# The gates of six groups computed after the scan in two-level block products, and the second stretch's layer norm in smaller steps

## The chip, the cores and the metric

The kernel runs on one core of a Trainium2 chip. The metric is the device time of one execution in microseconds. The core's engines run side by side and meet through semaphores: TensorE (PE, matmuls, with PEld for its weight loads), VectorE (DVE), ScalarE (ACT), GpSimd (POOL), and SyncE (SP), from which all of this kernel's transfers are issued in one queue.

## What is computed

A layer norm, then a Mamba-2 block and a LoRA mixture on the normed input, and the sum of all three. Everything is in fp32. With L = 2048 tokens and a model width of 1024, 64 heads of 64 channels, 8 groups:

```python
xn = layernorm(x)
proj = xn @ in_proj_w.T
gate, hbc, dt = proj[:4096], proj[4096:10240], proj[10240:]
xBC = silu(causal_conv4(hbc) + conv_bias)
x_, B, C = xBC                       # 64 heads x 64; 8 groups x 128 each
dt = softplus(dt + dt_bias); dA = exp(-exp(A_log) * dt)
state = state * dA_t + (dt_t * x_t) * B_t      # over t
y_t = state . C_t + D * x_t
yn = y * rsqrt(mean(y*y over a group's 512) + eps) * norm_weight
attn = (yn * silu(gate)) @ out_proj_w.T
ffn = xn @ W_base.T + b_base + 2 * lora(xn)    # 2 of 8 experts, rank 16
out = x + attn + ffn
```

The gate is a plain projection of the normed input: 4096 output channels, 512 of them per group. It is used only after the scan, as a factor on the normed y of the same channel and token.

## The kernel before

Channels lie on the 128 partitions, tokens along the free dimension. The tokens are cut into two stretches of 1024 (`s` = 0, 1); in `in_pairs` (line 557) each stretch's projections are computed in pairs of two 128-channel tiles by one level of Strassen-Winograd products. For the right-hand side (the normed input) the seven operands `op_0` to `op_6`, each 128 x (4 x 512), stay in SBUF for a whole stretch and are kept in DRAM as `xop_d`. `pair` (line 450) makes seven products of four matmuls 128 x 128 x 512; each fp32 matmul shows as two instructions. It is a generator that yields after each product: `products(n, side)` (line 591) advances it n times and runs the given side steps in between. After each product ACT or DVE evicts the bank: `s1` (line 474), `s16` (478), `s15` (482), and the four `quarter` calls (line 531 for the DVE ones), which store to DRAM. A bank `px` is written by products 6, 7 and 4, in the order 1, 6, 5, 2, 7, 3, 4. Left operands (weight sums) are formed on POOL in the first stretch (line 427), kept in DRAM and loaded again in the second.

A group has three pairs for the convolution's channels (names `x`) and two for the gate (`g`, evicted through SiLU to `gate_d`). The LoRA part's base product has four pairs per stretch (`b`). That makes 88 pairs in all, 616 products. The first five pairs run ahead, the last two (`POST`) after the scan.

The scan has 32 blocks (stretch, group, half of 512 tokens) of four slots (chunks of 128 tokens). The main loop (from line 983) sets how many products go into a slot by `plan` and `target`, a straight line through given points, and puts the scan's steps between them:

- `scan_a` for the next chunk: the decay scan `es` (DVE, line 688), the chunk's C.B product and transpose into bank "aux" (PE), the mask product `dab` (DVE, 709), the transposes of x into bank "aux" (PE, line 88), and `xdt`, `xdd` (ACT, 720 and 728; sixteen small instructions).
- `scan_b` for this chunk, after the slot's first product: `ps_y`, `ps_e`, `ps_st` (PE), `ecp` and `xg` (DVE, 769 and 770), the state's decay (POOL) and the state's sum (DVE, 784, from bank "st").
- `conv` for the next block in slots 1 and 2 (18 DVE instructions, line 646), `norm_squares` in slot 3, `norm_mean` and `norm_gate` in the next block's slot 0. `norm_gate` (line 818) multiplies by the gate (line 832; loaded in `load_gate`, line 791) and stores `y_d`.

The second stretch's input is normed during the first stretch, in four pieces of 256 tokens (`ln_next`, line 244, then `small`, line 297, for dt, decays and routing). A piece has three blocks. In the first of them it is loaded, normed and turned into operands within slots 1 to 3; `small` follows in slots of the other two. `ln_next` uses the four-buffer pool `ev`, which the evictions use too, and PSUM bank "st".

From block 15 on, POOL forms the output projection's weights for two levels (`out_sums`, line 866, from and to DRAM), one tile per block.

After the scan come the last two base pairs, and then the output projection (from line 1088): two levels of the same scheme. It has four passes (stretch, half of the groups) of seven units of seven products; here a product is eight matmuls of 256 columns. The stretches run in the order 1, 0. Right-hand quarters are loaded from `y_d`; sums for both levels are made on DVE.

Tiles are placed by a framework that inserts the semaphores; instructions marked `keep_in_program_order` (all matmuls and transposes among them) keep the order in which the code issues them.

Of the kernel before, what the change touches and what calls it, by code (L numbers as in the profile page):

```python
# [13 lines left out]
L = 2048  # L14
# [21 lines left out]
NW = 12  # L36
PRE = 5
# [5 lines left out]
def mamba_lora_kernel(  # L43
# [20 lines left out]
    const = ctx.enter_context(tc.tile_pool(name="const", bufs=1))  # L64
    in_ctx = ExitStack()
    op = in_ctx.enter_context(tc.tile_pool(name="op", bufs=1, side="right"))
# [177 lines left out]
    def ln_next(s, i):  # L244
# [4 lines left out]
        of = halved(flat, f"{s}_{i}", ev, "ev")  # L249
        yield  # L250
        ps = over_channels(of, "st", f"mean_{s}_{i}")
# [3 lines left out]
        sqs = []  # L255
        for h in range(2):
            normal(flat[:, 4 * h : 4 * h + 4, :], mean, ALU.subtract)
            for k in (4 * h, 4 * h + 2):
                sq = ev.tile([P, 2, 2 * Q], F32, tag="ev", name=f"lsq_{s}_{i}_{k}")
                nc.scalar.activation(sq, flat[:, k : k + 2, :], AF.Square)  # L260
                sqs.append(sq)
            nc.vector.tensor_tensor(sqs[2 * h], sqs[2 * h], sqs[2 * h + 1], ALU.add)
            if h:
                nc.vector.tensor_tensor(sqs[0], sqs[0], sqs[2], ALU.add)
            yield
        ps = over_channels([sqs[0][:, 0, :], sqs[0][:, 1, :]], "st", f"var_{s}_{i}")
# [4 lines left out]
        for h in range(2):  # L271
# [5 lines left out]
        t4, t1, t2, t3 = (  # L277
            ev.tile([P, KH, Q], F32, tag="ev", name=f"t_{s}_{i}_{j}") for j in range(4)
        )
        nc.vector.tensor_tensor(t1, b12, b11, ALU.subtract)  # L280
        nc.vector.tensor_tensor(t2, b22, t1, ALU.subtract)
        yield
        nc.vector.tensor_tensor(t4, b21, t2, ALU.subtract)
        nc.vector.tensor_tensor(t3, b22, b12, ALU.subtract)
# [12 lines left out]
    def small(s, i, chunks, sm, home):  # L297
# [7 lines left out]
        def tile(what, shape):  # L305
            pool, tag = home[what]
            return pool.tile(shape, F32, tag=tag, name=f"{what}_{n}")
# [25 lines left out]
        ps = ps_one.tile([P, nch, H], F32, tag="st", name=f"ps_tot_{n}")  # L333
# [223 lines left out]
    def in_pairs():  # L557
        for s in range(NS):
            ops = lambda s=s: ops_of["x", s]
            for g in range(G):  # L560
# [11 lines left out]
                for q in range(2):  # L572
# [14 lines left out]
    N_IN = NS * (5 * G + 4)  # L587
# [91 lines left out]
    def scan_a(s, g, half, c):  # L679
# [33 lines left out]
        pst = ps_one.tile([P, 4, Q], F32, tag="aux", name=f"ps_xt_{n}")  # L713
# [77 lines left out]
    def load_gate(s, g, half):  # L791
        sg = p1.tile([P, 4, TB], F32, tag="sg", name=f"sg_{s}_{g}_{half}")
# [25 lines left out]
    def norm_gate(s, g, half):  # L818
# [11 lines left out]
        for j in (0, 2):  # L830
            two = xg[:, j : j + 2, :]
            nc.vector.tensor_tensor(two, two, sg_of[s, g, half][:, j : j + 2, :], ALU.mult)
# [19 lines left out]
    def base_sums(pool, i):  # L852
# [7 lines left out]
        for j, what in ((3, "s1"), (4, "s2"), (5, "s3"), (6, "s4")):  # L860
            d = dram.tile([P, KH, P], F32, tag=f"{what}_b{i}", name=f"{what}_b{i}_d")
            nc.sync.dma_start(d, t[:, j])
            kept[f"b{i}", what] = d
        yield
# [107 lines left out]

    plan = [(0, 7 * PRE), (n_slots // 2 - NQ, 7 * (5 * G + 5)), (n_slots, total)]

# [433 lines left out]
```

## Time and profile before

| | us |
|---|---|
| median of three runs | 3438.68 (3438.17 to 3439.08) |
| the profiled execution | 3437.5 |
| its span, first to last instruction | 3435.7 |
| scan: first to last decay scan (L688) | 117.9 to 2644.9 |
| last one-level product begins | 2722.9 |
| first matmul of the output projection | 2726.3 |
| mean granted TensorE clock | 0.998 |

The span falls into a start of about 118 us, the scan of some 2530 us, the last base products, and the output projection of some 710 us. Transfers move 224 GB/s on average over the span. A busy time counts the stretches in which at least one instruction of the engine is under way; matmul instructions overlap, so the distance from one start to the next says more than the mean duration of one (592 ns for 512 columns). Waits are put down to what ended them last.

### The profile page before, as it was taken

Reading aid. Unit: us, or ns where it says so; the run is one execution under the profiler, and the core shown is the slowest. Engines: PE = TensorE matmul, PEld = TensorE weight load, DVE = VectorE, ACT = ScalarE, POOL = GpSimd, SP = SyncE. Lnnn points to the kernel's source line nnn. Section 1 sums busy time; section 2 is a strip of 40 time slices with the busy share of each in tenths; the row PEclk is TensorE's granted clock in tenths of the full one; section 3 lists DMA queues with packets and bytes.
Section 4 is the critical chain, followed back from the end, with each engine's and each line's share of the span. In section 5 each row is a group of like instructions: output and inputs, shape, how many; then the busy total and the mean of one; then the engine's idle time right before and its main releaser. Section 6 shows DMA issues by size and latency. Waiting matters only on the chain.

```text
span 3435.7 us, 38674 instructions
## 1 busy us (share of the span) xinstructions
PE 3404.6 (99%) x12820; PEld 1989.8 (58%) x12820; DVE 2410.5 (70%) x2733; ACT 1338.9 (39%) x3694; POOL 697.2 (20%) x443
## 2 busy tenths in 40 slices
PE   9999999999999999999999999999999999999999
PEld 7444544544545544544455454454454588888888
DVE  7547776877877867777777877777875466566665
ACT  2245454554555454545545455555453000000000
POOL 4123223222222211332222332222321000000000
PEclk9999999999999999999999999999999999999999
DMA  6546655655666676887778787877777777585654
GB/s 236 190 166 198 209 184 187 216 183 196 207 196 209 196 261 219 287 261 242 235 246 256 235 255 249 254 237 240 242 237 260 256 274 242 195 300 187 214 164 144
DMA packets 530327, 769.85 MB, mean 224 GB/s; under 512 B 35152, under 2 KB 264656, under 8 KB 527440
## 3 DMA queue, kind: packets, MB, share of 16 engines
q1 hardware_dynamic: 530128, 767.39, 68.7%
q8 instruction: 102, 1.67, 0.2%
q14 instruction: 97, 0.79, 0.1%
HBM read 516.64 MB, written 250.61 MB: 223 GB/s over the span
## 4 chain that ended last, share of the span: by engine, by line
PE 87%; DVE 8%; issue 2%; DMA 2%; ACT 2%; SPq 0%; DVEq 0%; ACTq 0%
PE ps_x_x L79 12%; PE ps_x_w L79 8%; PE ps_a_x L79 8%; PE ps_y_x L79 8%; PE ps_x_g L79 8%; PE ps_y_w L79 6%; PE ps_a_w L79 6%; PE ps_y_g L79 5%; PE ps_a_g L79 5%; PE ps_y L79 3%; PE ps_e L79 3%; PE ps_st L79 3%; PE ps_x_b L79 2%; DVE xg L646 2%; PE ps_a_b L79 2%
## 5 line engine op out<-in xcount | busy, mean ns | idle before, releaser
L83 POOL TENSOR_TENSOR state<-state,tot 128x512 f32<-128x512 f32 x112 | 150.2, 1341 | 1307.6 <-PE ps_e L79 1175.7
L688 DVE TENSOR_TENSOR_SCAN es<-dab,here 128x1024 f32<-128x1024 f32 x128 | 303.5, 2371 | 82.6 <-ACT xdd L728 81.3
L646 DVE SCALAR_TENSOR_TENSOR xg<-rawx,cw,xg 128x512 f32<-128x512 f32 x384 | 338.3, 929 | 16.8 <-ACT xg L640 15.9
L79 PE MATMUL ps_x_w<-t,w 128*128 128x256 f32 x1344 | 303.8, 379 | 0.0
L720 ACT ACTIVATE xdt<-ps_xt,dt 128x64 f32<-128x64 f32 x1024 | 223.0, 331 | 203.6 <-PE ps_xt L88 203.6
L79 PEld LDWEIGHTS ps_x_w<-t,w 128*128 128x128 f32 x1344 | 255.4, 190 | 41.5 <-issue 7.7
L705 ACT ACTIVATE ps_y<-xg,dsk 128x128 f32<-128x128 f32 x512 | 190.2, 371 | 222.5 <-DVE xg L770 192.9
L1345 ACT COPY s<-ps_a_w 128x512 f32<-128x512 f32 x28 | 16.4, 585 | 636.2 <-PE ps_a_w L79 555.6
L728 ACT ACTIVATE xdd<-xdt,es 128x64 f32<-128x64 f32 x1024 | 261.7, 387 | 0.0
L83 POOL TENSOR_TENSOR wo<-wo 128x512 f32<-128x512 f32 (+1 forms) x112 | 211.9, 1892 | 6.8
L709 DVE TENSOR_TENSOR dab<-es,cbm 128x1024 f32<-128x1024 f32 x128 | 177.6, 1388 | 39.3 <-ACT cbm L698 39.0
L79 PE MATMUL ps_a_w<-q,w 128*128 128x256 f32 x896 | 202.5, 379 | 0.0
L79 PEld LDWEIGHTS ps_a_w<-q,w 128*128 128x128 f32 x896 | 170.2, 190 | 23.6 <-issue 0.5
L79 PE MATMUL ps_x_x<-op_again,s_x 128*128 128x512 f32 x384 | 172.7, 592 | 0.0
L79 PE MATMUL ps_y_x<-op_again,s_x 128*128 128x512 f32 x384 | 172.7, 592 | 0.0
L79 PE MATMUL ps_a_x<-op_again,a_x 128*128 128x512 f32 x384 | 172.7, 592 | 0.0
L79 PEld LDWEIGHTS ps_y<-dab,xdt 128*64 128x64 f32 x2048 | 112.8, 137 | 102.9 <-issue 40.8
L79 PE MATMUL ps_x_x<-op,s_x 128*128 128x512 f32 x368 | 165.5, 592 | 0.0
L79 PE MATMUL ps_y_x<-op,s_x 128*128 128x512 f32 x368 | 165.5, 592 | 0.0
L79 PE MATMUL ps_a_x<-op,a_x 128*128 128x512 f32 x368 | 165.4, 592 | 0.0
L646 DVE SCALAR_TENSOR_TENSOR bc<-rawb,cw,bc 128x512 f32<-128x512 f32 x192 | 163.8, 885 | 1.9 <-ACT bc L640 1.3
L531 DVE TENSOR_TENSOR ev<-ps_x_x,s_x 128x512 f32<-128x512 f32 x94 | 64.4, 686 | 129.3 <-PE ps_x_x L79 124.2
(238 smaller groups left out, 6152.1 us busy)
## 6 DMA issues: line engine op xcount, KB each, us to landing
w<-w SPq DMA_DIRECT2D x196, 512.0 KB, 3.7
dab<-da_d SPq DMA_DIRECT2D x128, 512.0 KB, 5.4
raw<-ev SPq DMA_DIRECT2D x192, 256.0 KB, 3.3
a_x<-in_w_in_dram SPq DMA_DIRECT2D x168, 256.0 KB, 4.0
w<-wo SPq DMA_DIRECT2D x96, 448.0 KB, 4.3
ecp<-run_d SPq DMA_DIRECT2D x256, 128.0 KB, 4.0
gate<-ev SPq DMA_DIRECT2D x128, 256.0 KB, 3.6
sg<-gate SPq DMA_DIRECT2D x32, 1024.0 KB, 7.8
```

Source lines behind the costliest of these rows:

```text
L79: tc.keep_in_program_order(nc.tensor.matmul(*args, **kw))
L83: ins = nc.gpsimd.tensor_tensor(*args)
L531: nc.vector.tensor_tensor(e, ps, add, alu)
L646: nc.vector.scalar_tensor_tensor(dst[:, i, :], raw[:, i, k : k + TB], cw[:, ti, k : k + 1], dst[:, i, :], ALU.mult, ALU.add,)
L688: nc.vector.tensor_tensor_scan(es.rearrange("p h t -> p (h t)"), dab.rearrange("p h t -> p (h t)"), here, 0.0, ALU.mult, ALU.add,)
L705: nc.scalar.activation(psy[:, j, :], xg[:, j, cs], AF.Copy, scale=dsk[:, at : at + 1])
L709: nc.vector.tensor_tensor(ms, es, cbm.unsqueeze(1).to_broadcast([P, HG, Q]), ALU.mult)
L720: ins = nc.scalar.activation(xdt[:, h, :], x_t[:, h, :], AF.Copy, scale=dt_of[s][:, half * NQ + c, at : at + 1],)
L728: ins = nc.scalar.activation(xdd[:, h, :], xdt[:, h, :], AF.Copy, scale=es[:, h, Q - 1 : Q])
L1345: nc.scalar.copy(s1, pa)
```

## The change

It has two parts.

The first concerns the gates of groups 0 to 5 (`NO` = 3 pairs of groups). They leave `in_pairs`: 24 of the 88 pairs go, and `plan` is drawn anew for 64. `load_gate` does nothing for these groups, and `norm_gate` stores y without the gate. After the scan, during and behind the last base products, a new stage computes the gates: for each stretch and each two groups seven units (`gate_units`), each of them seven products of four matmuls of 256 columns. Left operands are read from `w_in` or from sums `s_d` that `oct_sums` forms on POOL, in blocks 30 and 31 and (the last third) in the new stage; the second level's left sums come from `left_two` (POOL), the right ones from `right_two` (DVE). The results gather in four tiles; `gated` applies SiLU (ACT), multiplies by y (DVE) and stores `yg_d`. The first stretch's operands are in place at the start; the second's are loaded again from `xop_d` towards the end of the first. The output projection then takes the stretches in the order 0, 1 and reads groups 0 to 5 from `yg_d`.

The second concerns the second stretch's layer norm. Each piece now takes twelve slots, from block 1 to block 12, with one or two steps per slot. It uses a scratch tile of its own (`scr`) in place of part of `ev`, and PSUM bank "aux" in place of "st"; `ps_xt`, the transposes of x in `scan_a`, moves from "aux" to "st". `out_sums` and the sums of the base weights begin one block earlier.

```diff
-                for q in range(2):
+                for q in range(2 if g >= 2 * NO else 0):
                     t = 4 * g + 2 * q
                     yield pair(
                         f"g{g}_{q}", f"g_{s}_{g}_{q}", halves(w_in[t], w_in[t + 1]), ops,
...
-        pst = ps_one.tile([P, 4, Q], F32, tag="aux", name=f"ps_xt_{n}")
+        pst = ps_one.tile([P, 4, Q], F32, tag="st", name=f"ps_xt_{n}")
...
-            nc.vector.tensor_tensor(two, two, sg_of[s, g, half][:, j : j + 2, :], ALU.mult)
+            if g >= 2 * NO:
+                nc.vector.tensor_tensor(two, two, sg_of[s, g, half][:, j : j + 2, :], ALU.mult)
...
-    plan = [(0, 7 * PRE), (n_slots // 2 - NQ, 7 * (5 * G + 5)), (n_slots, total)]
+    plan = [(0, 7 * PRE), (n_slots // 2 - NQ, 7 * (N_S + 4)), (n_slots, total)]
...
-            if after == 0 and c == 1:
+            i, at = divmod(4 * (b - 1) + c, 3 * NQ)
+            piece = (1, i)
+            if not (s == 0 and 0 <= i < NQ):
+                at = None
+            if at == 0:
                 load_piece(*piece, "sg", p1)
                 ln = ln_next(*piece)
-            if after == 0 and c == 2:
-                side += steps(ln, 3)
-            if after == 0 and c == 3:
-                side += steps(ln, 4)
-            if after == 1 and c in (0, 2, 3):
-                side += steps(rest, 1)
+            side += steps(ln, {2: 1, 3: 1, 4: 1, 5: 2, 6: 1}.get(at, 0))
+            side += steps(rest, {8: 1, 9: 1, 10: 1, 11: 2}.get(at, 0))
...
-            products(1, parts[3])
+            products(min(n - 3, 1), parts[3])
...
+    inner = (1, 6, 5, 2, 7, 3, 4)
+    HT = TB // 2
+    KQ = KH // 2
+    order = (1, 2, 6, 5, 7, 3, 4)
+    gate_units = [(s, o, i) for s in range(NS) for o in range(NO) for i in order]
...
+        add(s1, a21, a22, ALU.add)
+        yield
+        add(s2, s1, a11, ALU.subtract)
+        yield
+        add(s4, a12, s2, ALU.subtract)
+        yield
+        add(a21, a11, a21, ALU.subtract)
+        yield
...
+    def gated(s, o, a, n, z):
+
+        at = slice(s * TS + n * TB, s * TS + (n + 1) * TB)
+        y = gy.tile([P, 2, 2, TB], F32, tag="gy", name=f"gy_{s}_{o}_{a}{n}")
+        for q in range(2):
+            nc.sync.dma_start(y[:, q], y_d[2 * o + q][:, 2 * a : 2 * a + 2, at])
+        yield
+        for q in range(2):
+            nc.scalar.activation(z[:, q], z[:, q], AF.Silu)
+            yield
+        for q in range(2):
+            nc.vector.tensor_tensor(z[:, q], z[:, q], y[:, q], ALU.mult)
+            nc.sync.dma_start(yg_d[2 * o + q][:, 2 * a : 2 * a + 2, at], z[:, q])
+            yield
...
+        for n, j in enumerate(inner):
+            ps = {1: pa, 2: pa, 6: px, 7: px, 4: px, 5: py, 3: py}[j]
+            for q in range(2):
+                for k in range(KQ):
+                    mm(
+                        ps[:, q, :], left[j][:, q, k, :], right[j][:, k, :],
+                        start=(n < 3 and q + k == 0), stop=(k == KQ - 1), skip_group_check=True,
+                    )
...
-    passes = [(s, p) for s in (1, 0) for p in range(2)]
+    passes = [(s, p) for s in range(NS) for p in range(2)]
...
-            nc.sync.dma_start(x, y_d[4 * p + 2 * k + h][:, :, at : at + TB])
+            g = 4 * p + 2 * k + h
+            nc.sync.dma_start(x, (yg_d if g < 2 * NO else y_d)[g][:, :, at : at + TB])
```

## The prediction, made before the result was known

> **What bounds it now.** I read the busy shares first, then the order of matmuls on TensorE, then busy time in two stretches of the scan, then the waits.
>
> ```profile
> PE 3404.6 (99%) x12820; PEld 1989.8 (58%) x12820; DVE 2410.5 (70%) x2733; ACT 1338.9 (39%) x3694; POOL 697.2 (20%) x443
> ...
> 2667.09 3.60 PE L79 MATMUL ps_x_b<-op_again,s_b 128*128 128x512 f32 x8
> 2670.52 3.60 PE L79 MATMUL ps_y_b<-op_again,s_b 128*128 128x512 f32 x8
> ...
> 2729.77 3.62 PE L79 MATMUL ps_x_w<-t,w 128*128 128x256 f32 x16
> 2733.22 3.62 PE L79 MATMUL ps_y_w<-t,w 128*128 128x256 f32 x16
> ```
>
> PE is busy for 99% of the span, and products start one after the other without a gap: every 3.434 us for eight instructions of 512 columns, every 3.453 us for sixteen of 256. Only matmuls taken away, or gaps added, move the end. The second question is how much room the others have in the scan. The next lines are busy time by stretch: start:end, length, then PE, PEld, DVE, ACT, POOL, the granted clock, DMA share, GB/s.
>
> ```profile
> 340.10:1320.40 980.30, 969.90 (x3464) 496.22 (x3463) 735.02 (x936) 508.30 (x1378) 234.96 (x154) 1.00 0.63 206
> 1457.80:2535.00 1077.20, 1069.18 (x3892) 536.29 (x3892) 805.25 (x849) 558.21 (x1601) 300.01 (x167) 1.00 0.79 247
> ...
> 1718.00:1735.50 17.50, 17.50 (x68) 8.87 (x67) 14.48 (x14) 10.62 (x29) 1.04 (x1) 1.00 0.80 267
> 1735.50:1753.00 17.50, 17.50 (x68) 8.87 (x67) 17.30 (x20) 10.09 (x30) 8.29 (x5) 1.00 0.67 211
> 1753.00:1773.90 20.90, 20.90 (x76) 10.36 (x75) 11.43 (x11) 8.29 (x27) 10.93 (x5) 1.00 1.00 319
> 1773.90:1791.30 17.40, 17.40 (x66) 8.82 (x65) 10.59 (x15) 9.79 (x29) 0.00 (x0) 1.00 0.84 257
> ```
>
> The first row is 47 slots of the first stretch (11.75 blocks, with the layer norm), the second 58 slots of the second (14.5 blocks). The four rows below are one block, slots c = 0 to 3: 17.4 us with four products, 20.9 with five, so a slot is 3.72 us of scan matmuls plus 3.434 per product. DVE fills slot 1 (the convolution) and has room elsewhere.
>
> **TensorE's sum.** A one-level pair is 7 x 3.434 = 24.04 us; the 24 gate pairs of six groups are 576.9. A two-level unit is 56 instructions at 3.453/16 = 0.2158 us, 12.09 us; 2 x 3 x 7 = 42 units are 507.6. Difference: **-69.3 us**.
>
> Here a rule speaks against the change. The Trainium skill ("Perfetto Trace Analysis", Identifying the Most-Contended Engine) says that matmul busy share is a poor measure of nearness to the limit, and that the share of weight loading is a good one. The row: one weight load per matmul, 190 ns. The change drops 24 x 56 = 1344 loads (255 us) and adds 42 x 56 = 2352 (447 us). By the rule PE has half its time free in the scan (PEld 536 of 1077), so taking products away is worth nothing there, and the new stage at 190/216 = 88% is nearly at the limit: sum 0 or worse. By the row the products start back to back and the 190 ns lie under the 216, as through the whole output stage (PEld 608 of 709 us, PE 704). I take the row: -69.3.
>
> **The scan in shorter slots.** Products per slot fall from (315-35)/60 = 4.67 to (224-35)/60 = 3.15 in the first stretch and from 287/68 = 4.22 to 210/68 = 3.09 in the second: most slots become 3 products, 14.0 us. DVE loses five evictions of 0.686 us per pair and, in three blocks of four, two gate multiplies (2.37 us per block by their row). Per block:
> - First stretch: PE 969.9/11.75 = 82.5, less 6.07 products (20.8) = 61.7. DVE 735.0/11.75 = 62.6, less 0.87 pairs (3.0) and 1.8 = **57.8, 94%** of PE.
> - Second: PE 1069.2/14.5 = 73.7, less 4.53 products (15.6) = 58.1. DVE 805.3/14.5 = 55.5, less 2.2 and 1.8 = **51.5, 89%**. ACT is 38.5 before, still under two thirds.
>
> So DVE nearly becomes the bound. Slot 1 asks some 17 us of DVE in 14; the excess must run into slot 2. A late eviction hurts where product 4 overwrites the bank that product 7's eviction reads, one product (3.4 us) later. Spreading the layer norm over all twelve slots of a piece takes no instruction away. It moves DVE work out of the slots that now hold most of it (23.9 us of DVE in 904.8 to 932.0, a slot with five products) into the idle ones, and its one scratch tile leaves more of the four "ev" buffers to the evictions; I cost both at nothing. The price of a full DVE comes from slots of this trace in which it idles under 1 us:
>
> ```profile
> 683.10:700.50 17.40, 16.68 (x59) 7.97 (x58) 17.19 (x35) 6.69 (x14) 3.40 (x2) 1.00 0.47 168
> 864.70:883.00 18.30, 18.30 (x70) 9.58 (x69) 17.65 (x25) 9.65 (x28) 3.91 (x3) 1.00 0.54 174
> ...
> 1956.40:1975.40 19.00, 17.69 (x66) 8.74 (x65) 18.31 (x20) 11.00 (x31) 7.85 (x5) 1.00 0.72 217
> 2552.50:2569.90 17.40, 17.40 (x66) 8.82 (x65) 17.29 (x19) 10.86 (x30) 7.72 (x5) 1.00 0.81 233
> ```
>
> Eight such slots of the first stretch (from 360, 428, 615, 683, 865, 932, 1113 and 1181) lose 7.4 us of PE in all, 0.92 each; nine of the second (from 1587, 1661, 1736, 1809, 1956, 2032, 2401, 2476 and 2553) lose 3.9, 0.43 each. I let three of four slots be full in 12 blocks (3 x 0.92 x 12 = 33) and two of four in 16 (2 x 0.43 x 16 = 14). The stretches now lose 10.4 and 8.0, which this replaces: **+23 and +6**. Below: no stall at all, -18 together; above: the last rival.
>
> A stall above some 3 us costs more. The skill ("TensorE: Matmul & The Clock Gate", Part 1) has the clock halved after an idle window of about 3.4 us. The one stall here of that size, 4.6 us between 427.5 and 449.6, agrees: the granted clock is 0.97 in that slot and 0.89 in the next, 0.03 x 22.1 + 0.11 x 24.0 = 3.3 us more. My stalls are smaller pieces, so I add nothing; one such stall per piece of the layer norm would be 4 x 8 = 32.
>
> **Moved waits.** The transposes of x go from bank "aux" to "st", so they wait for the state add (DVE, 0.68 us) rather than for two ACT copies. Behind them on PE stands everything, but the add is issued some 7 us into the slot and the transposes come at 13.5, so it costs nothing until DVE is over 6 us late. The layer norm's sums go the other way, to "aux", and no longer stand before the state product. The SP queue loses 256 KB transfers of gate pairs and most gate loads; the scan's remaining loads are asked for one pair or two slots ahead.
>
> **The gate stage.** POOL: four adds per unit ahead by the 1.6 us row = 6.4 of 12.1 us. DVE: (4 x 5 + 3 x 9) evictions of 0.69 per seven units, 4.6 per unit; big adds 4 x 2.29/7 = 1.3; gating 8 x 1.22/7 = 1.4; right-hand differences 0.9: 8.2 of 12.1, 68%. The output stage runs at 446/709 = 63% and loses 4.9 us of PE in 28 units, 0.18 each; 42 units give **+8**. Bounds 0 and 25: product 4 now has 1.7 us, not 3.4, after product 7, and a 2.3 us add ahead of that eviction would show. DMA: 1 MB of weights and 8 MB/7 of y per unit, about 180 GB/s against 218 there: hidden. The gate pairs' own weight sums (12 pairs, 6.3 us of POOL each) leave the first stretch; the 12 new sums (48 POOL adds, 77 us) lie in the last two blocks, where POOL is a fifth busy, and beside units. Entering and leaving the stage: loads and the first operands are prepared under 48 us of base products, and the output stage's first 1 MB quarter (now of the first stretch, gated long before) needs tiles freed three units before the end: **+4**, between 0 and a bare load and two differences (7.4 + 2.4 = 10).
>
> Sum: -69.3 + 23 + 6 + 8 + 4 = -28. The profiled execution took 3437.5 us (span 3435.7), so 3409.5; the median of the runs lies 1.2 above it: **3411 us**.
>
> **Rivals.**
> 1. *The whole gain arrives* (backlog always fits into slots 2 and 3): -69.3 + 8 + 2 = -59, 3379. For: three full slots of the second stretch in a row of blocks (18 to 20) lose nothing. Against: 94%.
> 2. *DMA binds in the second stretch.* Share 0.79 of 74.3 us is 58.7 busy per block; 18.3 MB less 2.7 leaves 50, in 59 us: 85%. But slot 2 above is at 1.00 for 20.9 us while weight sums are stored, and shrinks to 14. A 1 us stall in each of 16 blocks gives 3427.
> 3. *DVE binds and the kernel gets slower.* Its queue is in order and idles behind others:
>
> ```profile
> DVE es L688 <- ACT xdd L728: 54.7, 24, 4.2
> DVE ev L531 <- PE ps_x_x L79: 47.3, 19, 6.6
> ```
>
> Let it idle x us per block. Then blocks take 57.8 + x and 51.5 + x, and the stalls are 12(x - 3.9) + 16(x - 6.6). They eat the gain (69.3 + 18.4 - 12 = 75.7) at **x = 8.2**. The least idle over four slots in a row here is about 10 to 11 (864.7 to 950.0: 85.3 less 74.2), though nobody pressed DVE then; my forecast needs 6.7 and 7.5. Midway, x = 9.2, gives +30: 3468.
>
> **Numbers.** Forecast 0.40 (3390 to 3428), rival 1 0.15, rival 2 0.10, near no change 0.06, rival 3 0.29. What can be told from no change is 0.2%, 7 us. Faster: 0.40 + 0.15 + 0.10 = 0.65; same 0.06; slower 0.29. The range leaves out the best end of rival 1 and the far end of rival 3: 3372 to 3470.
>
> **What would show it.** Right: scan blocks of 64 and 59 us with DVE over 85% busy and PE idle under 3 us; the gate stage 508 to 525 us at 0.216 us per instruction. Wrong: blocks near 67 and 61 us with PE waiting for evictions or for ACT's xdt; a 256-column spacing above 0.216; DMA at 1.00 over several slots with PE waiting for weights; or a hole over 10 us at either end of the gate stage.

## The result and the profile after

The change makes the kernel slower: 3520.2 us (median of four runs, 3510.87 to 3528.1) against 3438.63 in the same session, a ratio of 1.0236 (95% interval 1.0209 to 1.0263). The forecast was 3411, the upper end of its range 3470. The profiled execution of the changed kernel took 3523.57 us, its span is 3521.8, and its mean granted clock is 0.987 where it was 0.998.

Line numbers are now those of the changed kernel: matmuls L81, transposes L90, POOL's tensor operations L85, the decay scan L699, the convolution L657, the state's sum L795. First the busy shares of the page, then busy time by stretch (start:end, length; PE, PEld, DVE, ACT, POOL; clock, DMA share, GB/s): blocks 1 to 12, blocks 15 to 29, and the gate stage.

```profile
PE 3382.9 (96%) x13828; PEld 2200.4 (62%) x13828; DVE 2637.8 (75%) x2975; ACT 1339.6 (38%) x3677; POOL 975.4 (28%) x611
```

```profile
226.00:1014.00 788.00, 752.25 (x2968) 400.07 (x2965) 679.65 (x882) 477.88 (x1349) 191.86 (x123) 0.99 0.62 198
1148.00:2069.00 921.00, 885.12 (x3475) 457.40 (x3474) 787.00 (x809) 545.54 (x1597) 335.81 (x173) 0.99 0.83 256
2283.00:2810.00 527.00, 513.97 (x2352) 447.62 (x2351) 342.42 (x383) 85.00 (x114) 260.01 (x176) 0.99 0.61 207
```

PE is now without work for 3521.8 - 3382.9 = 138.9 us, before for 31.1. The clock costs 0.013 x 3521.8 = 45.8 us, before 0.002 x 3435.7 = 6.9. That is 146.7 us more lost; the span grew by 86.1, so the matmuls themselves became 60.6 us shorter. This counts an idle moment within a half-clock stretch twice. If half clock is counted only where PE is busy in the trace, it costs 35.5 us, before 4.4, and the matmuls became 52.8 us shorter. Either way the saving is there, and over twice as much was lost around it. A block takes 65.7 us in the first stretch and 61.4 in the second.

PE's waits (us in total, times, longest; `...` marks lines left out, here and in the code below):

```profile
PE ps_xt L90 <- DVE state L795: 31.4, 11, 6.7
PE ps_y L81 <- ACT xdt L731: 16.1, 7, 4.4
PE ps_x_b L81 <- DMA s_b<-s_b_d: 10.6, 1, 10.6
PE ps_e L81 <- ACT da L356: 10.5, 4, 4.9
PE ps_tot L81 <- DVE at L339: 8.4, 4, 3.0
...
PE ps_x_x L81 <- DVE ev L541: 6.2, 3, 4.1
PE ps_mean L81 <- DVE half L258: 5.6, 3, 3.4
```

No single wait makes the loss. The longest entry is the state's sum on DVE coming late; waits around the small products of the layer norm and of `small` (da, tot, mean) make 24.5 us. (`ps_da` and the scan's `ps_e` use the same bank, so `ps_e` waits for the copy of `ps_da`.) Evictions, which the forecast named, make 6.2 in their longest entry and under 10 in all.

Where it was lost is read best by stage. The next table (not a view of the profile) is worked out from the starts and ends of the matmuls and the granted clock in each trace: length of the stage in us, and in brackets the time lost in it, idle PE plus half of each stretch at half clock (so with the double count just named). Blocks are cut at their first decay scan; "end" is blocks 30 and 31 with the base products behind them, and "output" reaches to the last matmul. As a measure of its spread: the first stretch loses 46 to 48 us in all seven other kernels with the same steps there (e2, e5, e9 to e13), the second 38 to 46 in those with the same steps there (e2, e7, e8). The table holds the runs of the experiments too.

| kernel | 1-12 | 13-14 | 15-29 | end | gates | output |
|---|---|---|---|---|---|---|
| before | 1003 (14) | 157 (0) | 1117 (8) | 211 (0) | | 704 (0) |
| **after** | 788 (46) | 134 (13) | 921 (46) | 214 (46) | 527 (16) | 707 (2) |
| e6_short | 821 (85) | 116 (2) | 945 (68) | 181 (8) | | 704 (0) |
| e1_banks | 787 (46) | 130 (18) | 936 (56) | 215 (48) | 522 (11) | 707 (2) |
| e7_oldln | 799 (62) | 140 (21) | 914 (38) | 212 (47) | 524 (14) | 707 (3) |
| e8_late | 795 (54) | 132 (10) | 918 (42) | 211 (44) | 525 (14) | 708 (3) |
| e10_phase | 789 (48) | 131 (12) | 913 (39) | 215 (49) | 528 (16) | 706 (2) |
| e2_nosums | 787 (48) | 134 (14) | 924 (46) | 173 (3) | 527 (15) | 706 (2) |
| e3_lessdve | 771 (31) | 125 (3) | 896 (28) | 212 (40) | 525 (14) | 707 (2) |
| e5_noout | 788 (47) | 121 (8) | 876 (2) | 211 (40) | 529 (18) | 708 (3) |
| e9_noadds | 788 (47) | 126 (9) | 901 (28) | 217 (48) | 527 (16) | 707 (3) |
| e12_poolq | 788 (46) | 132 (17) | 928 (50) | 207 (37) | 522 (11) | 708 (3) |
| e11_moved | 788 (46) | 121 (8) | 897 (20) | 175 (0) | 611 (107) | 707 (3) |
| e13_both | 787 (46) | 121 (8) | 908 (31) | 174 (0) | 603 (96) | 707 (3) |
| e14_all | 771 (31) | 119 (2) | 875 (3) | 174 (0) | 524 (14) | 706 (2) |
| e15_no2 | 867 (47) | 135 (3) | 1003 (41) | 188 (0) | 353 (13) | 709 (4) |
| e16_no1 | 927 (39) | 152 (6) | 1048 (11) | 201 (0) | 183 (12) | 707 (1) |

### The profile page after: what moved, and what is told of

It reads as the page before. It is cut to its first block, busy times and chain, and to the rows that moved or that the text cites. A ratio compares the mean times of both kernels' runs of the same rounds, so it can differ in the third digit from the quotient of the medians.

```text
span 3521.8 us, 41174 instructions
## 1 busy us (share of the span) xinstructions
PE 3382.9 (96%) x13828; PEld 2200.4 (62%) x13828; DVE 2637.8 (75%) x2975; ACT 1339.6 (38%) x3677; POOL 975.4 (28%) x611
## 3 DMA queue, kind: packets, MB, share of 16 engines
q1 hardware_dynamic: 535360, 796.75, 69.3%
## 4 chain that ended last, share of the span: by engine, by line
PE 69%; DVE 13%; DMA 7%; ACT 4%; issue 4%; POOL 2%; SPq 1%; DVEq 0%; POOLq 0%; ACTq 0%
PE ps_x_x L81 8%; PE ps_x_w L81 8%; PE ps_a_x L81 6%; PE ps_y_x L81 6%; PE ps_a_w L81 5%; PE ps_y_w L81 5%; PE ps_x_z L81 5%; PE ps_a_z L81 3%; PE ps_y_z L81 3%; DVE xg L657 3%; PE ps_e L81 2%; PE ps_y L81 2%; PE ps_st L81 2%; PE ps_x_g L81 2%; PE ps_x_b L81 1%
## 5 line engine op out<-in xcount | busy, mean ns | idle before, releaser
L85 POOL TENSOR_TENSOR state<-state,tot 128x512 f32<-128x512 f32 x112 | 161.0, 1437 | 918.9 <-PE ps_e L81 875.3
L699 DVE TENSOR_TENSOR_SCAN es<-dab,here 128x1024 f32<-128x1024 f32 x128 | 322.2, 2517 | 83.1 <-ACT xdd L739 59.8
L657 DVE SCALAR_TENSOR_TENSOR xg<-rawx,cw,xg 128x512 f32<-128x512 f32 x384 | 339.8, 929 | 22.0 <-ACT xg L651 21.1
L81 PE MATMUL ps_x_w<-t,w 128*128 128x256 f32 x1344 | 303.8, 379 | 0.0
L81 PEld LDWEIGHTS ps_x_w<-t,w 128*128 128x128 f32 x1344 | 255.4, 190 | 41.5 <-issue 6.9
L85 POOL TENSOR_TENSOR wo<-wo 128x512 f32<-128x512 f32 (+1 forms) x112 | 239.6, 2139 | 16.8 <-DMA ecp<-run_d 9.9
L81 PE MATMUL ps_a_w<-q,w 128*128 128x256 f32 x896 | 204.2, 381 | 3.1 <-DMA w<-w 3.1
L720 DVE TENSOR_TENSOR dab<-es,cbm 128x1024 f32<-128x1024 f32 x128 | 168.7, 1318 | 48.0 <-ACT cbm L709 47.8
L81 PEld LDWEIGHTS ps_y<-dab,xdt 128*64 128x64 f32 x2048 | 118.0, 138 | 118.5 <-ACT xdd L739 74.3
L81 PEld LDWEIGHTS ps_a_w<-q,w 128*128 128x128 f32 x896 | 171.2, 191 | 27.3 <-issue 3.8
L437 POOL TENSOR_TENSOR s_x<-a_x,a_x 128x512 f32<-128x512 f32 x48 | 76.2, 1587 | 354.3 <-PE ps_x_x L81 121.6
L81 PE MATMUL ps_y<-dab,xdt 128*64 128x128 f32 x2048 | 150.7, 284 | 23.4 <-ACT xdt L731 16.1
L81 PE MATMUL ps_x_x<-op_again,s_x 128*128 128x512 f32 x384 | 173.0, 593 | 0.0
L81 PE MATMUL ps_y_x<-op_again,s_x 128*128 128x512 f32 x384 | 172.7, 592 | 0.0
L81 PE MATMUL ps_a_x<-op_again,a_x 128*128 128x512 f32 x384 | 172.7, 592 | 0.0
L81 PE MATMUL ps_y_x<-op,s_x 128*128 128x512 f32 x368 | 169.0, 603 | 2.5 <-DVE s_x L492 2.5
L81 PE MATMUL ps_x_x<-op,s_x 128*128 128x512 f32 x368 | 165.5, 592 | 0.0
L81 PE MATMUL ps_a_x<-op,a_x 128*128 128x512 f32 x368 | 165.5, 592 | 0.0
```

The source lines that it names most:

```text
L81: tc.keep_in_program_order(nc.tensor.matmul(*args, **kw))
L85: ins = nc.gpsimd.tensor_tensor(*args)
L437: nc.gpsimd.tensor_tensor(t[what], t[x], t[y], alu)
L657: nc.vector.scalar_tensor_tensor(dst[:, i, :], raw[:, i, k : k + TB], cw[:, ti, k : k + 1], dst[:, i, :], ALU.mult, ALU.add,)
L699: nc.vector.tensor_tensor_scan(es.rearrange("p h t -> p (h t)"), dab.rearrange("p h t -> p (h t)"), here, 0.0, ALU.mult, ALU.add,)
L720: nc.vector.tensor_tensor(ms, es, cbm.unsqueeze(1).to_broadcast([P, HG, Q]), ALU.mult)
```

## Experiments

The theories at the start: (1) the exchange of banks puts the transposes behind a late state sum; (2) DVE, nearly full in short slots, is late by itself; (3) the new weight sums at the end of the scan, and the transfers and POOL work they bring, hold back the scan's own steps.

**e1_banks: only the exchange of banks undone.**

```diff
-        pst = ps_one.tile([P, 4, Q], F32, tag="st", name=f"ps_xt_{n}")
+        pst = ps_one.tile([P, 4, Q], F32, tag="aux", name=f"ps_xt_{n}")
...
-        ps = over_channels(of, "aux", f"mean_{s}_{i}")
+        ps = over_channels(of, "st", f"mean_{s}_{i}")
```

> The changed kernel with the bank swap undone: the transposes of x go to bank aux again, the layer norm's sums, ps_tot and ps_sm to st. Theory 1 (the moved bank): in the changed kernel the transposes wait 31 us in 11 places for the state add, which stands behind POOL's state decay and so behind POOL's weight sums; after it come late xdt and half-clock stretches. Undone, 50 to 70 us go: 3450 to 3470. Theory 2 (DVE is full, whatever the bank): at most the 31 us go and others come in their place: 3490 to 3515. Theory 3 (sums of the last blocks): about 20 us less, since the state add late there no longer holds the transposes: 3495.

3529.75 us, ratio 1.0263 (1.0233 to 1.0293): not faster. The first wait of PE, in the same view, has a new owner:

```profile
PE ps_xt L90 <- ACT bt L711: 50.5, 19, 6.5
```

Theory 1 falls. The bank was not the cause; in the old bank the transposes wait for ACT's copy, and longer.

**e6_short: the kernel before with the six groups' gate pairs left out**, and their groups not gated. It has the short slots and nothing else of the change.

```diff
-                for q in range(2):
+                for q in range(2 if g >= 6 else 0):
```

> The kernel before with nothing but its six groups' gate pairs left out (24 pairs of TensorE work, 576.9 us; y of these groups goes on ungated). Bank, layer norm, weight sums and tail are as before. If the changed kernel's losses come from slots of 14 us as such, this one loses 60 to 85 us as well: 2925 to 2945 instead of 2862. If they come from the change's own pieces (bank swap, fine layer norm, sums in blocks 30 and 31), it comes within 20 us: 2862 to 2882.

2998.29 us. Without any new loss it would be 3438.7 - 576.9 = 2862, so 136 us of the matmuls' time did not come out, more than either forecast had. Reckoned as above the matmuls are 576.6 us shorter, just the 24 pairs (569.8 without the double count), and the rest is idle PE and clock: 85 us in blocks 1 to 12, 68 in blocks 15 to 29. Short slots do this with nothing else of the change, without the gate stage or the new sums at the end, and more than in the changed kernel. So the rest of the change helps the scan, but not enough; of the 39 us between 85 and 46, the next run gives 16 to the finer layer norm. What brings the others was not separated.

**e7_oldln: the layer norm in its old rhythm** (within one block, three and four steps per slot), everything else as in the changed kernel.

```diff
-            side += steps(ln, {2: 1, 3: 1, 4: 1, 5: 2, 6: 1}.get(at, 0))
+            side += steps(ln, {2: 3, 3: 4}.get(at, 0))
```

> The changed kernel with the layer norm's steps in the old rhythm: load and all of ln_next within slots 1 to 3 of a piece's first block, small in slots 3 to 8. If the fine steps help, as the prediction had it, blocks 1 to 12 lose more than their 36 us idle and 10 us of clock: 3535 to 3560. If PE's waits for the layer norm (ps_mean, ps_tot, ps_da) come from the fine steps, 20 to 30 us go: 3490 to 3505.

3530.28 us, ratio 1.0268 (1.0238 to 1.0298), less than the first forecast had. Over the whole kernel the interval overlaps that of the changed kernel, so no gain is shown there; in blocks 1 to 12, where the steps lie, 62 us are lost instead of 46.

**e8_late: one step of `small`, the sum of the decays and their transposes, one slot later.**

```diff
-            side += steps(rest, {8: 1, 9: 1, 10: 1, 11: 2}.get(at, 0))
+            side += steps(rest, {8: 1, 10: 2, 11: 2}.get(at, 0))
```

> The changed kernel with one step of small moved: the sum over tokens and the transposes (ps_tot, ps_da) come two slots after the DVE chain that feeds them instead of one. If those waits (8.4 us for ps_tot, 10.5 for ps_e behind ps_da's copy) come from a chain that is simply not done after one short slot, they go, with half their clock loss: 3490 to 3505. If DVE is full and the chain is late by whatever there is, nothing changes: 3515 to 3525.

3523.37 us, ratio 1.0248 (1.0218 to 1.0277), no change that these intervals can show. PE's wait for the sum of the decays (tot, 8.4 us) went, and its wait for ACT's xdt grew instead.

**e2_nosums: the sums of blocks 30 and 31 left out**; units of the first two pairs of groups then read plain weights, so the gates of these four groups are not the reference's.

```diff
-            if b in (30, 31):
-                left_sums = oct_sums(wo, "wo", b - 30, c)
-                next(left_sums)
```

> The changed kernel without the weight sums of blocks 30 and 31: the gate units of the first two group pairs read plain weight blocks in their place, so their gates are not the reference's. Theory 3 (those sums stop the chain from POOL to the state and hold up the SP queue): the 18 us of waits from 2139 to 2203, the 10.6 us wait for base weights at 2260 and their half-clock stretches go: 3480 to 3490. Theories 1 and 2: 3500 to 3515, for only a fifth of the idle time lies there.

3482.66 us (3482.48 to 3482.84), ratio 1.0126: 38 us less, all of it at the end of the scan (46 to 3). The changed kernel's order of events there shows how these sums do it (start us, us, engine line op out<-in xcount, idle before and its releaser):

```profile
2122.27 0.32 SPq L164 DMA_DIRECT2D op_again<-xop  x1
2122.63 1.38 SPq L892 DMA_DIRECT2D ws<-in_w_in_dram  x3
2129.35 0.33 SPq L164 DMA_DIRECT2D op_again<-xop  x1
...
2132.76 5.28 POOL L85 TENSOR_TENSOR ws<-ws 128x512 f32<-128x512 f32 x4 [20.83 <-DMA ws<-in_w_in_dram]
2134.05 4.34 SPq L901 DMA_DIRECT2D s<-ws  x4
2137.99 1.04 POOL L85 TENSOR_TENSOR state<-state,tot 128x512 f32<-128x512 f32 x1
2139.07 0.69 DVE L795 TENSOR_TENSOR state<-state,ps_st 128x512 f32<-128x512 f32 x1 [8.43 <-POOL state L85]
2139.82 1.12 PE L90 MATMUL ps_xt<-ident,xg 128*128 128x128 f32 x4 [6.73 <-DVE state L795]
```

The loads of `ws` stand in SP's queue between loads of the operands (`op_again`), each of which waits for a product on PE. POOL's additions, issued ahead of the state's decay, wait for them 20.83 us; the decay stands behind in POOL's queue, DVE's state sum waits for the decay, the transposes for the sum. The place in SP's queue is only half of those 20.83 us. The last three loads are issued from 2122.63 on and land at 2131.3 to 2132.6, some 9 us later, while the DMA engines were full (DMA share 1.02 in this row, columns as above):

```profile
2118.00:2133.00 15.00, 14.64 (x58) 7.30 (x56) 6.41 (x8) 10.41 (x32) 0.24 (x1) 1.00 1.02 405
```

POOL is busy for 69 of the 215 us at the end of the scan, a third, and the slot was lost all the same. Theory 3 holds for this place. Of the 33 us that PE idles there, four such waits make 16; the wait for `s_b` in the list above, 10.6 us, is another, for a load of base weights that stands in SP's queue behind stores of the same sums.

**e3_lessdve: reciprocal and four scalings of `norm_gate` left out** (the norm of y is not applied): 3.35 + 4 x 0.745 = 6.3 us of DVE per block.

```diff
-        nc.vector.reciprocal(std, std)
...
-            nc.vector.scalar_tensor_tensor(
-                xg[:, j, :], xg[:, j, :], nw[:, 4 * g + j : 4 * g + j + 1], std,
```

> The changed kernel without the reciprocal and the four scalings of norm_gate (6.2 us of DVE per block, 26 us per four blocks; y is left unscaled). Theory 2 (a full DVE makes the stalls): DVE falls under 85% of PE's time in both stretches and most stalls go: 3400 to 3430. Theory 1: the waits of the transposes behind POOL stay: 3470 to 3500. Theory 3: 3490 to 3510.

3470.67 us, ratio 1.0091 (1.0062 to 1.0121): 50 us less, from 46 to 31 and from 46 to 28 in the two stretches. DVE's load matters, but theory 2 wanted 3400 to 3430: a tenth of DVE's work brings back a third of what the scan loses. (3470 was also the edge of what theory 1 forecast, which e1_banks had ruled out.)

**e5_noout: the sums of the output weights in blocks 14 to 29 left out**, loads, additions and stores; the output stage reads other data.

```diff
-            left_sums = out_sums(wo, b - 14)
+            left_sums = iter([None] * 4)
```

> The changed kernel without the output projection's weight sums in blocks 14 to 29 (the output projection reads other data of the same shape in their place; the sums of blocks 30 and 31 stay). If POOL's sums, their loads and stores hold up the state and the SP queue in the second stretch, its 36 us of idle PE and 12 us of half clock fall to under 10 together: 3475 to 3490. If the slots are simply too short for the chain of a slot, or DVE is full, they stay: 3505 to 3525.

3464.06 us, ratio 1.0075 (1.0046 to 1.0104): 56 us less, and blocks 15 to 29 lose 2 us instead of 46. The first stretch, where no such sums stand, loses what it did. That is more than the forecast had. So in the second stretch short slots and DVE's own work do not make the loss by themselves; it takes these sums beside them. The groups of DVE over blocks 15 to 29 (line, shapes, count; busy, mean ns; idle before), in the changed kernel:

```profile
L657 DVE SCALAR_TENSOR_TENSOR xg<-rawx,cw,xg 128x512 f32<-128x512 f32 x180 | 175.7, 1023 | 8.7 <-ACT xg L651 8.2
L699 DVE TENSOR_TENSOR_SCAN es<-dab,here 128x1024 f32<-128x1024 f32 x61 | 159.4, 2613 | 45.6 <-DMA dab<-da_d 23.2 <-ACT xdd L739 22.3
```

and in e5_noout:

```profile
L699 DVE TENSOR_TENSOR_SCAN es<-dab,here 128x1024 f32<-128x1024 f32 x61 | 141.5, 2319 | 37.6 <-ACT xdd L739 37.6
L657 DVE SCALAR_TENSOR_TENSOR xg<-rawx,cw,xg 128x512 f32<-128x512 f32 x180 | 126.9, 756 | 4.1 <-ACT xg L651 3.5
```

The same convolution instruction takes 1023 ns on average in the stretch with POOL's additions and 756 in the one without. It is no new slowing: the kernel before has these sums too, and there the average over blocks 15 to 29 is 980.

```profile
L646 DVE SCALAR_TENSOR_TENSOR xg<-rawx,cw,xg 128x512 f32<-128x512 f32 x180 | 168.0, 980 | 3.2 <-ACT xg L640 2.7
```

New is that the slot is too short to hide it. One slot of the changed kernel in order of time:

```profile
1917.68 0.74 DVE L657 SCALAR_TENSOR_TENSOR xg<-rawx,cw,xg 128x512 f32<-128x512 f32 x1
...
1922.67 7.82 DVE L657 SCALAR_TENSOR_TENSOR xg<-rawx,cw,xg 128x512 f32<-128x512 f32 x5
...
1924.93 2.52 POOL L85 TENSOR_TENSOR wox<-wo 128x896 f32<-128x896 f32 x1
...
1927.53 8.90 POOL L85 TENSOR_TENSOR wo<-wo 128x896 f32<-128x896 f32 x3
...
1930.41 4.15 DVE L699 TENSOR_TENSOR_SCAN es<-dab,here 128x1024 f32<-128x1024 f32 x1
...
1935.78 0.68 DVE L795 TENSOR_TENSOR state<-state,ps_st 128x512 f32<-128x512 f32 x1
...
1936.52 1.12 PE L90 MATMUL ps_xt<-ident,xg 128*128 128x128 f32 x4 [4.78 <-DVE state L795]
```

Alone a convolution step takes 0.74 us; five beside POOL take 7.82, 1.56 each, and the decay scan 4.15 instead of 2.3. What then comes late is the state's sum behind them in DVE's queue, and PE waits 4.78 us.

**e9_noadds: only POOL's additions for these sums left out**, loads and stores kept (of loaded parts).

```diff
-        level_one_sums(t)
-        store(0, t[:, :, 0])
+        store(0, 0)
...
-        add(t[:, :, 2], t[:, :, 2], t[:, :, 3], ALU.add)
```

> The changed kernel with POOL's additions for the output weights left out, their loads and stores kept (the stores write loaded parts, so the output weights' sums are not the reference's). If the second stretch loses its time because DVE runs beside POOL's additions: its idle falls from 36 to under 12 us and the time is 3468 to 3485. If the transfers, or stores that stand in SP's queue, are what it waits for: 3510 to 3525, idle over 28 us there.

3498.2 us, ratio 1.0174 (1.0159 to 1.0189), between the two forecasts: blocks 15 to 29 lose 28, where it was 46 with the additions and 2 without the transfers too. The convolution is back at 764 ns, so POOL's additions are what stretched it. What remains comes with the transfers. ACT's first entry over these blocks in e9_noadds, and the same entry in the changed kernel, are

```profile
ACT xg L651 <- DMA y<-xg: 75.0, 14, 11.2
ACT xg L651 <- DMA y<-xg: 27.7, 12, 5.2
```

against 19.7 us in e5_noout: in e9_noadds the convolution starts late because the store of the y before it, which frees its buffer, is late. In the changed kernel this wait is hardly longer than without the sums. Each store is cut in two in e9_noadds and waits for no addition, so part of its 28 us may be of its own making; how much of the changed kernel's 46 the transfers cost is not shown.

**e12_poolq: the stores of all these sums on POOL's own DMA queue.**

```diff
-            nc.sync.dma_start(w2_d[p][:, j, :, q, kt, :].rearrange("i c o -> c i o"), src)
+            nc.gpsimd.dma_start(w2_d[p][:, j, :, q, kt, :].rearrange("i c o -> c i o"), src)
```

> The changed kernel with one thing altered: the stores of the output weights' sums and of the last blocks' sums go out on POOL's own DMA queue, behind the additions they wait for, instead of standing in SP's queue in front of other loads. If the stores in SP's queue are what delays the loads of the last blocks and half of the second stretch (transfers cost 25 us there beyond the additions): last blocks and tail fall from 46 us of idle and clock loss to under 20, the second stretch from 46 to 20 to 30, 3465 to 3490. If POOL's additions beside DVE are all of it, or issuing on POOL costs as much: 3510 to 3530.

3516.32 us, ratio 1.0229 (1.0212 to 1.0246): the first forecast missed. Blocks 15 to 29 lose 50, the end 37 instead of 46. Moving the stores gained nothing that these intervals show. Either they are not what delays the scan, or issuing them on POOL costs as much: there an issue takes POOL 0.56 us and more, ahead of the state's decay. The loads behind `op_again` stay where they were in this kernel.

**e10_phase: the odd product of each block in slot c = 1.**

```diff
+        base, full = evenly(NQ * b_), evenly(NQ * b_ + NQ)
+        return base + 3 * c_ + 3 + min(c_, full - base - 12) if c_ < NQ - 1 else full
```

> The changed kernel with the same products per block, but the slots dealt so that the odd product of a block always stands in slot c = 1, where the convolution is. If the short slot with the convolution is what starts the stalls: 3495 to 3510, with less idle in both stretches. If DVE's load over the whole block sets them: 3515 to 3527, no change.

3511.36 us, ratio 1.0207 (1.019 to 1.0224): between the two forecasts. The second stretch loses 39 instead of 46, the first 48. Which slot gets the fourth product matters little, and no difference is clear of the intervals.

**e11_moved and e13_both: the sums dealt otherwise**, half of the output weights' sums in every second block, half beside gate units, those of the last blocks in blocks 16 to 23; in e13_both their stores on POOL's queue as well.

```diff
-        if summing:
-            left_sums = out_sums(wo, b - 14)
+        if summing and b % 2 == 0:
+            outs = out_sums(wo, (b - 14) // 2)
...
+            for k in range(8):
+                gen = out_sums(gt, 8 + k)
```

> The changed kernel with the weight sums dealt otherwise: half of the output weights' sums in the second stretch, in slots c = 3 and c = 2 of every second block, with each store one slot behind its additions; the other half beside gate units; the sums of the first two pairs of groups in blocks 16 to 23 instead of the last two. If POOL's additions and the stores that wait for them make the losses: last blocks and tail lose under 8 us instead of 46, the second stretch about 25 instead of 46, 3455 to 3475. If the gate stage pays it back, where POOL would be 10.5 of 12.1 us busy per unit: its idle goes from 13 to over 30 us, 3480 to 3500.

> The sums dealt as in the run where half of the output weights' sums lie beside gate units (3527.5 us, of which 107 were lost in the gate stage), with their stores on POOL's queue. If stores that wait in SP's queue made the gate stage late: its idle falls from 76 to under 25 us and the time is 3440 to 3465. If POOL at 10.5 of 12.1 us per unit slows DVE and holds the operands back: idle stays over 50 there, 3500 to 3525.

3527.5 and 3530.54 us, ratios 1.026 (1.0245 to 1.0275) and 1.0265 (1.025 to 1.0281), slower than any of the forecasts. The scan does what was hoped (13-14 at 8, 15-29 at 20, the end at 0), and the gate stage gives all of it back: 107 us lost instead of 16. Its row in e11_moved, columns as above:

```profile
2206.00:2817.00 611.00, 534.91 (x2354) 457.73 (x2352) 390.61 (x387) 86.99 (x115) 412.15 (x240) 0.95 0.73 234
```

POOL is busy for 412 us of 611 there and DVE for 391, where the changed kernel's same stage had 260 and 342. PE waits for POOL's operands and for DVE's partial sums. With stores on POOL's queue it is nearly the same (96), with the same reservation as for e12_poolq.

**e14_all: e2, e5 and e3 together**, with the same parts left out.

> The three partial omissions in one kernel: no sums in the last two blocks, no output-weight sums in the second stretch, and no reciprocal and no four scalings per block (what reads these sums reads other weights, and the norm is not applied). One by one they gave 38, 56 and 50 us. If they are separate causes that add up and the matmul term of -69 is right: 3370 to 3385. If they share one cause (any relief would have done): 3425 to 3450. If the matmul term itself is short: over 3390 with under 15 us of idle left.

3400.81 us, ratio 0.9889 (0.9872 to 0.9905): 119 us less than the changed kernel, where the three alone make 144. This is 16 us above the forecast for separate causes and well below that for one cause. In the first stretch and at the end they add up; in the second, e3 and e5 bring back the same time (28 and 2 alone, 3 together). The page and the two stretches:

```profile
PE 3344.9 (98%) x13828; PEld 2186.0 (64%) x13828; DVE 2366.5 (70%) x2815; ACT 1338.9 (39%) x3677; POOL 672.8 (20%) x451
```

```profile
224.00:995.00 771.00, 747.18 (x2973) 399.37 (x2970) 613.17 (x822) 475.71 (x1349) 203.72 (x123) 0.99 0.62 204
1114.00:1989.00 875.00, 872.14 (x3469) 452.20 (x3468) 623.35 (x734) 545.09 (x1595) 81.90 (x54) 1.00 0.60 195
```

Its clock is 0.996, so 53.8 + 13.6 = 67.4 us are lost, 29.4 more than before, and the span is 37.0 shorter: the matmuls are 66.4 us shorter (65.1 without the double count).

**e15_no2 and e16_no1: smaller doses**, four and two groups behind the scan, their sums in blocks 16 to 23 and 16 to 19, and the layer norm in its old rhythm (its tile is needed for gates otherwise).

```diff
-NO = 3
+NO = 2
...
+        if 16 <= b < 16 + 4 * NO:
+            octs = oct_sums(p1, "sg", (b - 16) // 4, b % 4)
```

> Four groups instead of six behind the scan (28 units), the sums of their weights in blocks 16 to 23, the layer norm in its old rhythm; everything else as in the changed kernel. Matmuls alone: -46 us against before. If losses grow out of too short slots and go quickly as slots get longer (3.7 products instead of 3.1): 3425 to 3450. If they come from the sums and the transfers beside the scan whatever the slots: the second stretch still loses 40 or more, 3460 to 3490.

> As the run with four groups, with two (14 units): matmuls alone -23 us against before, some 4.2 and 3.8 products per slot. If the losses go with the length of the slots: 3420 to 3440, losses of the scan under 35 us. If the sums beside the scan set them: 3450 to 3470.

3492.14 us, ratio 1.0154 (1.0139 to 1.0169), and 3457.36, ratio 1.0053 (1.0038 to 1.0068). By their times both are near the second forecast, but the stages split it. With four groups blocks 15 to 29 still lose 41; with two they are nearly whole again (11), with the same output sums beside them: slots long enough do hide them. But blocks 1 to 12 lose 47 and 39, where the kernel before loses 14, and the gate stage 13 and 12; with the rest of the scan that is more than the 46 and 23 us of matmuls taken away. Part of the loss in blocks 1 to 12 may come from the layer norm's old rhythm here (e7_oldln). Neither smaller dose gained. In e15_no2 the reckoning leaves 31 us of matmul saving where 46 were due; that gap stays open.

**e17_beforebank: the kernel before with the exchange of banks alone.**

```diff
-        pst = ps_one.tile([P, 4, Q], F32, tag="aux", name=f"ps_xt_{n}")
+        pst = ps_one.tile([P, 4, Q], F32, tag="st", name=f"ps_xt_{n}")
```

> The kernel before with the exchange of PSUM banks alone: the transposes of x in the bank of the state product, the layer norm's sums in the other. If the exchange frees the transposes of ACT's copies in long slots too: 5 to 9 us of the 27 us that the kernel before loses to idle and half clock come back, 3429 to 3434. If in long slots nothing waits for this bank: 3437 to 3440.

3437.93 us, ratio 0.9998 (0.999 to 1.0006): no difference. In long slots nothing waits for that bank. No kernel with the whole computation beat the one before. The layer norm's part of the change alone (e4_lnonly, all gates as before) gave no time: by the code, each block would wait for its gate in the tile that the layer norm's piece holds over several blocks, and the program comes to a standstill.

## Why the prediction was wrong

The profiled execution took 3523.6 us where 3409.5 had been reckoned for it, 114 more. By its trace some 33 of them are idle PE at the end of the scan, 30 are idle time in blocks 13 to 29 beyond the 14 that I had priced, 31 are half clock while PE was busy, 16 are matmuls that did not shrink as far as reckoned, and a few lie elsewhere. The step that failed is the price of the scan in shorter slots, in three of its terms: the second stretch, the sums of the last blocks, and the clock.

**TensorE's sum, -69.3: nearly right.** The reckoning gives 52.8 to 60.6 us in the changed kernel and 65.1 to 66.4 in e14_all; what the stalls add to the rest is open. An instruction of the gate stage takes 513.97/2352 = 0.2185 us at a clock of 0.99, so 0.216 at full clock. The rule on weight loads that I set aside would have given nothing.

**"First +23": right for idle, by luck.** PE idles 35.7 us in blocks 1 to 12; the forecast was 33. But evictions are not what it waits for (1.3 us there): the waits around the layer norm's small products, 24.5 us, all lie in these blocks. "I cost both at nothing", of the finer steps, missed a gain of 16 us in these blocks (e7_oldln).

**"Second +6": wrong, 36 us idle.** DVE's duration was forecast well: 51.5 us per block, and it came out at 787.0/15 = 52.5, with 8.9 us of idle per block. What failed is the price of a full DVE, 0.43 us a slot, taken from nine slots of the trace before. The additions of POOL that stood in the same slots before were hidden by slots of four and five products (e16_no1, with slots of nearly four, loses only 11 beside them); in slots of three the late steps show. e5_noout takes the loss to 2, e9_noadds to 28. The Trainium skill ("SBUF — State Buffer", Who interferes with whom) says that a DVE instruction with two SBUF inputs contends with a GpSimd instruction that reads SBUF. The convolution step is one; 0.74 against 1.56 us is its size here. The average of 980 ns before holds it already: the mean was in my figures, and what I missed is that the slow steps fall together in one slot.

**"They lie in the last two blocks, where POOL is a fifth busy": put at nothing, 38 us (e2_nosums).** Busy share was the wrong question. The sums stand in POOL's queue ahead of the state's decay, and their loads in SP's queue behind loads that wait for products, in blocks where the DMA engines are full for part of the time. The prediction asked of PE's queue what stands behind a waiting instruction, and did not ask it of POOL's and SP's.

**"My stalls are smaller pieces, so I add nothing": wrong by 31 to 39 us.** (Part of this lies in the terms above.) I took the idle window of about 3.4 us (the Trainium skill, "TensorE: Matmul & The Clock Gate", Part 1) as a threshold for one stall. In the trace stalls of 1.9 us can halve the clock (below). Nor were the pieces small: of the 7.4 us in my eight slots of the first stretch, 4.6 are the one stall behind which the prediction itself shows a halved clock.

**The moved wait** heads PE's list, but undoing it gained nothing (e1_banks). **The gate stage, +8 and +4:** 527 us stand against 507.6 + 12 = 519.6, and 16 us are lost in it; near enough.

**Rivals.** Rival 3 had the scan nearly to the point: DVE idles 9.0 and 8.9 us per block, break-even was put at 8.2, the rival's 9.2 gave 3468. The measured times of 65.7 and 61.4 us per block are also what the prediction gave as the sign of being wrong (67 and 61). By its formula, 12 x (9.0 - 3.9) + 16 x (8.9 - 6.6) = 98 us of stalls; blocks 1 to 29 lose 46 + 13 + 46 = 105 with the clock. But that idle was not queueing alone: POOL beside DVE, transfers and the layer norm's chain had a part in it. What takes 3468 on to 3520 is mostly the end of the scan, 46. Rival 2 may have a part in the second stretch: without POOL's additions e9_noadds still loses 26 us more there than without the transfers, but with the reservation made above. At the end of the scan the DMA engines were full where it hurt.

What stays open is the first stretch: in e14_all it still loses 31 us, and no run here took that away. Its waits there are again mostly those around the steps of `small` (`ps_e` 11.1 us, `ps_tot` 6.8, of 24 us idle).

## What to carry to other kernels

When work is taken out of a slot, what it hid comes up. Price it slot by slot: a mean over the stretch was right here to 2%, and hid that the slow steps fall together. For every step that is put into a queue, ask on each engine that it uses, POOL and SP too, what waits behind it and what it waits for itself; a low busy share says nothing about that. A smaller dose is worth a run, but expect it to keep the fixed costs.

## What the runs showed of the hardware

The clock halves after stalls much shorter than expected, and not after all of them. Three stretches in the gate stage of the changed kernel (columns: start:end, length, PE busy, granted clock, DMA share, GB/s): a stall of 1.9 us, the next 1.4 us, and then 3.4 us.

```profile
2489.50:2491.40 1.90, 0.06 (x1) 1.00 0.85 290
2491.40:2492.80 1.40, 1.40 (x5) 0.72 0.86 317
2492.80:2496.20 3.40, 3.40 (x11) 0.61 0.53 199
```

And a stall of 3.4 us in the first stretch, after which the clock stays whole:

```profile
861.90:865.30 3.40, 0.06 (x1) 1.00 0.62 231
865.30:868.70 3.40, 3.40 (x29) 1.00 0.27 88
```

The trace's clock record has 18 such half-clock stretches in scan, gate stage and output, of 3.4, 6.8 or 10.2 us. They all begin on one grid of 3.413 us. If PE's idle time is added up window by window on that grid, what decides comes out of the trace: all 20 windows with 2 us or more of idle are followed by a window at half clock, 3 of the 8 with 1.7 to 2 us, 4 of the 42 with 0.5 to 1.7, and none of the 276 with less. (In the 18 traces of this case together: 303 of 305, 37 of 71, 59 of 595, none of 17234.) The stall of 1.9 us lay whole in one window; the one of 3.4 us was cut by the grid into 1.97 and 1.38. So the price of a stall of 2 to 3 us is 0 or 1.7 us on top, depending on where it falls; with many stalls a quarter to a third on top of the idle time (46 on 128 us within those stages, less if half clock counts only where PE is busy).

DVE's slowing beside POOL is by a factor of two in one slot, and gone in e9_noadds (764 ns).
